# A four-layer graph-attention kernel: which products share a PSUM bank in layer 1, and in which round layer 2 takes a tile's last products

## The chip, the cores and the metric

The kernel runs on one core of a Trainium2 chip. The metric is the device time of one execution in microseconds (us); one measurement of this kernel is the median over several executions. The core has five engines with instruction streams of their own: TensorE (PE, with its weight loads shown apart as PEld), VectorE (DVE), ScalarE (ACT), GpSimd (POOL) and SyncE (SP). SP, ACT and POOL also issue DMA transfers. [...]

## The reference

Four graph layers act on `x` with 4096 nodes of 256 features. The adjacency matrix is sparse: each pair of nodes is joined with a chance of about 0.1% in either direction, made symmetric, with a loop at every node, so that a node has some nine neighbours. Each layer is residual and starts with a layer norm and a relu:

```python
h = jnp.maximum(_layernorm(x, axis=-1), 0.0)
x = x + layer(h, adj, ...)
```

- Layer 0: `h @ W.T` in 8 heads; a softmax over the neighbours of `leaky_relu(e_l[i] + e_r[j])` plus a bias from curvature features; the weighted sum of the neighbours' rows.
- Layer 1: one head. `e = a1·h[i] + a2·h[j]`, leaky relu, softmax over the neighbours, weighted sum of the neighbours' rows.
- Layer 2: as layer 1, but with two softmaxes, one over `e` and one over `-e`. Both weighted sums of the rows are concatenated, multiplied with `wtrans` (512x256) and passed through elu.
- Layer 3: four heads of 64 features. `h = x @ W + b`, the score of a pair is `leaky_relu(h[i]·h[j])`, absent edges score 1.0 and stay in the softmax; then relu.

## The kernel before, in words

**Tiles and lists.** The 4096 nodes are 32 tiles of 128 rows. A first stage turns the adjacency matrix into lists. For every tile there are nine chunks of 128 neighbour rows (`EC`), and one-hot matrices `st` that say which edge goes to which row of the tile. A layer keeps one row per node in a table in DRAM (`table0` to `table3`), which holds what the next layer needs of a node.

**Gathers.** The function `run` (L1698) works a layer through, tile by tile. For each tile POOL issues one indirect DMA for each chunk (`gather`, L914), which fetches 128 rows of the table into the buffer `g`. Six buffers exist (L827), so POOL runs up to six tiles ahead of the products that read them. The tile's own 128 rows come by an ordinary DMA from SP. The lists are sorted so that the first seven chunks touch the first 28 tiles' rows only (`NE` = 3584): these "early" gathers of the next layer can start when the rows of tiles 0 to 27 are in the table. The remaining chunks are "late" and need the whole table. In layers 1 and 3 the last chunk isn't gathered: TensorE expands it from rows kept in SBUF (`expanded`, L1682), with a one-hot matrix `to`, twelve matmuls and a copy by ACT into `g` (L1692). So POOL issues 9 gathers a tile in layers 0 and 2, and 8 in layers 1 and 3.

**Rounds.** `run` is given a list of steps, each with a lag. In round r, a step with lag k handles tile r - k; in a round the steps stand in the order of the list. TensorE executes in exactly this order. The instructions of the other engines are put in order by a scheduler, each engine's queue then being fixed in the program.

**Layer 1.** Its steps are: `loads` of tile r+3, which calls `go_to`; then gathers; `give2` of tile r-3; `weigh1` of r; `finish1` of r-2; `attend1` of r-1 (`summed`, L934 to L943, which frees the buffer `g`); `turn2` and `rows2` of r-2; `before1` of r+1; `expand1` of r+1. The small products are these. `go_to` (L1674) spreads a column of indices over 128 columns in PSUM, which DVE compares with row numbers (L1677) to give `to`. `give` (L908 in `to_edges`) sends a tile's own coefficients to its edges: nine matmuls of 3 columns, which DVE sums up (L1752). It is called for layer 1's coefficients (`before1`) and for layer 2's (`give2`). The PSUM tile "pm" of `ps_m` (one buffer) takes both `give`s; the tile "pe" of `ps_e` (one buffer) takes `go_to` and `expanded`. A PSUM tile is one bank, and a user waits for the last reader of the user before.

**Layer 2.** For a tile t, `weigh2` makes the two weight matrices (DVE L1872 and around), `attend2` multiplies them with `g` (28 matmuls a tile, L1894), `signed2` scales, `turn_signed` and `through_wt` multiply with `wtrans` (L1916, L1929), `finish2` gives the new `x` and its centred row `r`. Then come a tile's last products: `turn3` transposes `r` (L863) and ACT copies it to `hT` (L865); `rows3` multiplies `hT` with layer 3's weights (four matmuls, L872), DVE forms the row (L1957), and after every second tile ACT issues a store of two tiles' rows to `table3` (`store_two`, L774). `rows3` also splits the row in three bfloat16 parts, stores them in `own3`, and sums up squares on ACT (L1970). The order in a round is: `weigh2` of r, `signed2` of r-1, `finish2` of r-2, `attend2` of r, `turn3` of r-2, `turn_signed` of r-1, `rows3` of r-2, `before2` of r+1, `through_wt` of r-1.

**Layer 3.** POOL's queue first holds 42 early gathers (seven for each of the first six tiles), then late ones. The first of all waits for the store of tiles 26 and 27 to `table3`. `weigh3` needs all chunks of its tile (L2025, L2031, L2052, L2064), and `attend3` (again `summed`, L934 to L943) frees the buffer for the seventh tile's gathers.

Of the kernel before, what the change touches and what calls it, by code (L numbers as in the profile page):

```python
# [20 lines left out]
P = 128  # L21
# [675 lines left out]
EC = 9  # L697
# [16 lines left out]
def gnn_lists(  # L714
# [29 lines left out]
    NT = N // P  # L744
# [77 lines left out]
    own = [const.tile([P, NT, 3], F32, name=f"own{i}") for i in (1, 2)]  # L822
# [32 lines left out]
    def bank(pool, name, dtype=F32):  # L855
        t = pool.tile([P, 512], F32, name=name)
        return t if dtype == F32 else t.bitcast(dtype)
# [18 lines left out]
    def upper(a):  # L876

        n = len(a.shape)
        two = a.bitcast(BF16)
        if n == 2:  # L880
            return two.rearrange("p (a two) -> p a two", two=2)[:, :, 1]
        return two.rearrange("p s (a two) -> p s a two", two=2)[:, :, :, 1]
# [22 lines left out]
    def to_edges(pe, st, parts):  # L905

        for c in range(EC):
            nc.tensor.matmul(  # L908
                pe[:, c, :], lhsT=st[:, c * P : (c + 1) * P], rhs=parts, start=True, stop=True
            )  # L910
# [43 lines left out]
    with tc.tile_pool(name="keep", bufs=1) as keep, tc.tile_pool(  # L954
# [97 lines left out]
        at = keep.tile([P, NT], F32, name="at")  # L1052
# [573 lines left out]
    with tc.tile_pool(name="work", bufs=2) as work, tc.tile_pool(name="kept", bufs=1) as kept, tc.tile_pool(  # L1626
# [10 lines left out]
        def s_chunks(st):  # L1637

            pt = ps_s.tile([P, EC + 7, P], BF16, name="s_ps")[:, :EC, :]
            for c in range(EC):  # L1640
                nc.tensor.transpose(pt[:, c, :], st[:, c * P : (c + 1) * P], ident_b)  # L1641
            return pt
# [6 lines left out]
        def weights():  # L1649
            return work.tile([P, 2 * (HC + 2) * P], F32, name="sw")  # L1650
# [6 lines left out]
        def in_parts(parts, row, rest):  # L1657
            nc.scalar.copy(parts[0], row)
            nc.vector.tensor_sub(rest, row, parts[0])
            nc.scalar.copy(parts[1], rest)  # L1660
            nc.vector.tensor_sub(parts[2], rest, parts[1])

        def keep_late(rows, width):

            for b in range(0, LB, 2):
                n = min(LB, b + 2) - b
                row = rows[b // 2 - (LB + 1) // 2][:, 2 - n :, :]
                rest = work.tile([P, 2, ROW1], F32, name="rest", bufs=1)[:, :n, :width]
                in_parts([late_rows[:, b : b + n, i, :width] for i in range(3)], row, rest)

        def go_to(t, to):

            pm = bank(ps_e, "pe")[:, :P]
            nc.tensor.matmul(  # L1674
                pm, lhsT=col_late[:, t : t + 1].to_broadcast([P, P]), rhs=ident, start=True, stop=True
            )
            nc.vector.tensor_tensor(  # L1677
                to.rearrange("p (b e) -> p b e", b=LB), pm[:, None, :].to_broadcast([P, LB, P]),
                late_no[:, :, None].to_broadcast([P, LB, P]), op=OP.is_equal,
            )  # L1680

        def expanded(t, of, width, pool, name):  # L1682

            to = of.pop("to")
            ps = bank(pool, name)[:, :width]
            for b in range(LB):
                for i in range(3):
                    nc.tensor.matmul(  # L1688
                        ps, lhsT=to[:, b * P : (b + 1) * P], rhs=late_rows[:, b, i, :width],
                        start=(b == 0 and i == 0), stop=(b == LB - 1 and i == 2),  # L1690
                    )
            nc.scalar.copy(of["g"][:, LATE, :width], ps)  # L1692

        def store_x(dst, t, of):
            if t % XT == XT - 1:
                store(rows_of_x(dst, t + 1 - XT), of.pop("all_x"))
# [48 lines left out]

        a2_of = kept.tile([P, NT, EC + 1], F32, name="a2_of")

        def give(a, st, own_t):

            pe = bank(ps_m, "pm")[:, : EC * 3]  # L1750
            to_edges(pe.rearrange("p (c s) -> p c s", c=EC), st, upper(own_t))
            nc.vector.tensor_reduce(a[:, :EC], pe.rearrange("p (c s) -> p c s", c=EC), AX.X, OP.add)  # L1752
            nc.scalar.copy(a[:, SELF:], own_t[:, 0:1])

        def scores(g, a):
            s = work.tile([P, EC + 1], F32, name="s")
            with ExitStack() as queue:
                for step in behind.values():
                    queue.enter_context(tc.issue_after(step.ins))
                nc.vector.tensor_add(s, g[:, :, C + 1], a)  # L1760
            nc.vector.scalar_tensor_tensor(s, s, 0.2, s, op0=OP.mult, op1=OP.max)
            return s

        with tc.tile_pool(name="l1_o", bufs=2, space=PSUM) as ps_o, tc.tile_pool(
            name="l1_t", bufs=2, space=PSUM
        ) as ps_t, tc.tile_pool(name="l1_e", bufs=1, space=PSUM) as ps_e:
            for b in range(LB):
                nc.vector.tensor_scalar(
                    late_no[:, b : b + 1], number, float(NE + b * P), None, op0=OP.add
                )  # L1770
            nc.vector.tensor_copy(col_late, nbr[:, :, LATE])
            keep_late([rows12[t // 2 % len(rows12)] for t in range(0, NT, 2)], ROW1)

            def expand1(t, of):
                expanded(t, of, ROW1, ps_e, "pe")

            def before1(t, of):
                a = of["a"] = work.tile([P, EC + 1], F32, name="a")
                give(a, of["st"], own[0][:, t, :])
                of["s"] = s_chunks(of["st"])  # L1780

            def give2(t, of):
                give(a2_of[:, t, :], of.pop("st"), own[1][:, t, :])

            def weigh1(t, of):
                s = scores(of["g"], of.pop("a"))
                w = work.tile([P, EC + 1], F32, name="w")
                nc.scalar.activation(w, s, AF.Exp)
                sw = of["sw"] = weights()[:, : (EC + 1) * P].rearrange("p (c r) -> p c r", r=P)
                nc.vector.tensor_mul(  # L1790
                    sw[:, :EC, :], of.pop("s"), w[:, :EC, None].to_broadcast([P, EC, P])
                )
                nc.vector.tensor_scalar(
                    sw[:, SELF, :], ident, w[:, SELF:], loop[:, t : t + 1], op0=OP.mult, op1=OP.mult
                )

            def attend1(t, of):
                sw, g = of.pop("sw"), of.pop("g")
                o = of["o"] = bank(ps_o, "o")[:, : C + 1]
                summed(o, sw, g, C + 1, [(sw[:, SELF, :], g[:, SELF, : C + 1])])  # L1800

            def finish1(t, of):
                o, x = of.pop("o"), of.pop("x")
                nc.vector.reciprocal(inv[1][:, t, :], o[:, :1])
                nc.vector.scalar_tensor_tensor(
                    x, o[:, 1:], inv[1][:, t, :], x, op0=OP.mult, op1=OP.add
                )
                nc.vector.tensor_add(x, x, bias1)
                of["r"], of["rstd"] = normed(work, x)
                store_x(xs[1], t, of)  # L1810

            def turn2(t, of):
                of["hT"] = transposed(work, ps_t, of["r"])

            def rows2(t, of):
                rstd = of.pop("rstd")
                row = rows12[t // 2 % len(rows12)][:, t % 2, :]
                nc.scalar.activation(row[:, 1 : C + 1], of.pop("r"), AF.Copy, scale=rstd)
                pp = times(ps_t, of.pop("hT"), wcat2, 2)
                nc.vector.tensor_scalar(row[:, C + 1 :], pp[:, :1], rstd, None, op0=OP.mult)  # L1820
                nc.vector.tensor_scalar(own[1][:, t, 0:1], pp[:, 1:], rstd, None, op0=OP.mult)
                if t % 2:
                    store_two(table2, t, rows12[t // 2 % len(rows12)])
                split_own(own[1], t, 1)

            run(
                table1, ROW1, xs[0],
                [
                    (3, give2), (0, weigh1), (2, finish1), (1, attend1), (2, turn2), (-1, before1),
                    (2, rows2), (-1, expand1),  # L1830
                ],
                first=True, expand=True,
            )
# [15 lines left out]
        with tc.tile_pool(name="l2_o", bufs=1, space=PSUM) as ps_o, tc.tile_pool(  # L1849
# [93 lines left out]

            rows3_of = []

            def turn3(t, of):
                of["hT"] = transposed(work, ps_t, of.pop("r"))

            def rows3(t, of):
# [19 lines left out]
                for k in range(K3):  # L1969
# [4 lines left out]
            run(  # L1974
                table2, ROW1, xs[1],
                [
                    (0, weigh2), (1, signed2), (2, finish2), (0, attend2), (2, turn3), (1, turn_signed),
                    (2, rows3), (-1, before2), (1, through_wt),
                ],
            )  # L1980

# [213 lines left out]
```

## Time and profile before

| what | us |
|---|---|
| median of 14 runs | 1616.87 (1610.12 to 1620.17) |
| the profiled execution's own time | 1618.42 |
| its span | 1616.7 |
| first gather of layer 1, 2, 3 | 524.2, 853.33, 1217.54 |
| last gather of layer 2 | 1215.68 |
| last gather of layer 3 | 1554.89 |

The profile is of one execution, and all its times count from the start of the span; 1.7 us of the execution's time lie around it. An engine's group of instructions is given by line, operation, and tiles, with busy time and the idle time before it. "issue" as the cause of an idle time means that the engine waited for nothing that the profile shows. For an indirect DMA, POOL's bar is the time to issue it; the data land later. The mean clock granted to TensorE was 0.876 of full speed.

### The profile page before, as it was taken

The page shows a single profiled execution, that of the slowest core. Times are in us where ns is not written, and L with a number is a line of the kernel's source. Part 1 is how long each engine was busy: PE and PEld are TensorE (multiplying, and loading weights), DVE is VectorE, ACT ScalarE, POOL GpSimd, SP SyncE. Part 2 cuts the span into 40 slices and gives each one's busy share as a digit, 9 for nine tenths or more (in the row PEclk, how much of TensorE's full clock was granted, in tenths as well). Part 3 has the DMA queues.
Part 4 walks back from the last instruction along what each step waited for, and adds up shares of the span by engine and source line. Part 5 has one row for each costly group of instructions (what it writes and reads, how often), then busy time and mean ns, then how long its engine had stood idle before and what let it go on. Part 6 is the DMA issues. An engine that isn't in the chain of part 4 may idle for free.

```text
span 1616.7 us, 28902 instructions
## 1 busy us (share of the span) xinstructions
PE 1271.9 (79%) x9569; PEld 929.5 (57%) x9584; DVE 1091.1 (67%) x2979; ACT 763.5 (47%) x2246; POOL 1057.0 (65%) x1145
## 2 busy tenths in 40 slices
PE   4674788877888649988874499999997588888885
PEld 3342455545556337665553488888886355555553
DVE  5666778788877547765643266777665477888885
ACT  4565667776454334433321044444444344554543
POOL 2027766765666767777777777777777577777730
PEclk9975877787789769989796799999998699999998
DMA  8879888998556747877676467677767456666620
GB/s 267 293 246 321 286 287 288 324 306 255 131 150 170 221 138 226 242 204 198 205 228 183 127 195 206 194 210 213 207 207 214 147 175 196 195 205 198 212 78 16
DMA packets 167342, 338.02 MB, mean 209 GB/s; under 512 B 31761, under 2 KB 103697, under 8 KB 167185
## 3 DMA queue, kind: packets, MB, share of 16 engines
q0 software_dynamic: 52224, 145.30, 33.9%
q1 hardware_dynamic: 67714, 134.54, 24.8%
q10 hardware_dynamic: 47246, 56.27, 10.0%
q8 instruction: 77, 1.26, 0.3%
q14 instruction: 81, 0.66, 0.1%
HBM read 282.22 MB, written 53.77 MB: 208 GB/s over the span
## 4 chain that ended last, share of the span: by engine, by line
PE 31%; DMA 6%; POOL 6%; issue 5%; DVE 5%; ACT 2%; DVEq 0%; ACTq 0%; POOLq 0%; SPq 0%
PE o L1894 11%; DMA g<-table,nbr 6%; POOL g L914 6%; PE o L934 4%; PE pv L2025 3%; PE pt L1929 3%; PE o L939 3%; DVE v L2031 2%; PE pt L872 2%; PE o L943 1%; PE s_ps L1641 1%; PE pt L1916 1%; ACT y L2081 1%; PE pe L1688 0%; PE pt L863 0%
## 5 line engine op out<-in xcount | busy, mean ns | idle before, releaser
L914 POOL DMA_INDIRECT g<-table,nbr x1088 | 1042.4, 958 | 406.3 <-issue 308.9
L1894 PE MATMUL o<-g,sw 128*128 128x257 f32 x896 | 201.4, 382 | 36.6 <-DVE sw L1872 35.4
L1894 PEld LDWEIGHTS o<-g,sw 128*128 128x128 f32 x896 | 170.6, 191 | 62.0 <-DVE sw L1872 35.7
L2025 PE MATMUL pv<-parts,st 64*128 64x256 bf16 (+1 forms) x864 | 93.9, 288 | 67.4 <-DVE v L2031 65.4
L1192 ACT ACTIVATE mask<-adj,minus_half 128x1024 bf16<-128x1024 int32 x112 | 125.1, 1142 | 14.7 <-DMA adj<-in_adj_l 5.1
L2025 PEld LDWEIGHTS <-st 64*128 64x128 bf16 (+1 forms) x864 | 57.3, 99 | 101.0 <-issue 93.8
L2081 ACT ACTIVATE y<-o,inv 128x64 f32<-128x64 f32 x128 | 36.0, 312 | 164.1 <-DVE inv L2077 164.1
L872 PE MATMUL pt<-wcat,hT 128*128 128x272 f32 (+2 forms) x384 | 95.0, 365 | 13.8 <-ACT hT L865 11.8
L2031 DVE TENSOR_TENSOR v<-pv,g 128x512 f32<-128x512 f32 (+1 forms) x160 | 93.2, 630 | 17.9 <-DMA g<-table,nbr 12.3
L939 PE MATMUL o<-g,sw 128*64 128x257 f32 (+1 forms) x768 | 102.0, 402 | 0.0
L865 ACT COPY hT<-pt 128x256 f32<-128x256 f32 x128 | 46.9, 367 | 112.8 <-PE pt L863 109.4
L896 ACT ACTIVATE off<-place,minus 128x1152 bf16<-128x1152 f16 x64 | 80.0, 1251 | 37.5 <-DVE st L897 36.9
L1641 PE MATMUL s_ps<-ident_b,st 128*128 128x128 bf16 x864 | 66.7, 225 | 36.2 <-DVE sw L1790 36.2
L863 PE MATMUL pt<-ident,r 128*128 128x128 f32 x256 | 56.1, 305 | 46.1 <-DVE r L843 15.0
L1531 DVE TENSOR_TENSOR g<-g,pb 128x2560 f32<-128x2560 f32 x32 | 90.0, 2813 | 3.4 <-ACT pb L1528 3.3
L2064 DVE TENSOR_TENSOR g<-g,pm 128x2048 f32<-128x2048 f32 x32 | 73.2, 2288 | 25.8 <-ACT pm L2057 25.7
L934 PE MATMUL o<-g,sw 128*128 128x257 f32 (+1 forms) x320 | 89.6, 414 | 0.0
L1688 PEld LDWEIGHTS <-st 128*128 128x128 bf16 x768 | 80.3, 109 | 15.3 <-issue 1.6
L1641 PEld LDWEIGHTS <-st 128*128 128x128 bf16 x864 | 56.7, 100 | 46.3 <-DVE sw L1790 24.0
L2052 DVE TENSOR_REDUCE s<-v 128x36 f32<-128x2304 f32 x32 | 81.7, 2553 | 1.1
L872 PEld LDWEIGHTS pt<-wcat,hT 128*128 128x128 f32 x384 | 65.0, 204 | 28.9 <-ACT hT L865 16.3
L1499 ACT CAST s_f<-pt 128x1024 f32<-128x1024 bf16 x64 | 37.8, 642 | 92.8 <-PE o L943 92.4
(363 smaller groups left out, 2716.5 us busy)
## 6 DMA issues: line engine op xcount, KB each, us to landing
adj<-in_adj_l SPq DMA_DIRECT2D x128, 512.0 KB
g<-table,nbr POOLq DMA_INDIRECT x1088
rows_of<-st ACTq DMA_DIRECT2D x16, 832.0 KB
st<-rows_of SPq DMA_DIRECT2D x16, 832.0 KB
x<-x SPq DMA_DIRECT2D x24, 512.0 KB
st<-rows_of SPq DMA_DIRECT2D x16, 576.0 KB
table<-row ACTq DMA_DIRECT2D x32, 258.0 KB
g<-table SPq DMA_DIRECT2D x64, 129.0 KB
```

The costliest lines, as they stand in the source:

```text
L872: nc.tensor.matmul(pp, lhsT=hT[:, k, :], rhs=w[:, k, :], start=(k == 0), stop=(k == KC - 1))
L914: nc.gpsimd.indirect_dma_start(out=g[:, c, :width], out_offset=None, in_=table[: NE if c < EARLY else N, :], in_offset=bass.IndirectOffset ...
L934: nc.tensor.matmul(o, lhsT=a, rhs=b, start=(i == 0), stop=False)
L939: nc.tensor.matmul(o[rows], lhsT=s[:, c + h * HC, rows], rhs=g[:, c + h * HC, :width], start=False, stop=False,)
L1192: nc.scalar.activation(m, a, AF.Sign, bias=minus_half, scale=1.0)
L1531: nc.vector.tensor_mul(gh, gh, w[:, :, :, None].to_broadcast([P, K, H0, D0]))
L1641: nc.tensor.transpose(pt[:, c, :], st[:, c * P : (c + 1) * P], ident_b)
L1688: nc.tensor.matmul(ps, lhsT=to[:, b * P : (b + 1) * P], rhs=late_rows[:, b, i, :width], start=(b == 0 and i == 0), stop=(b == LB - 1 and i ...
L1894: nc.tensor.matmul(o, lhsT=sw[:, h, i].rearrange("p s r -> p (s r)"), rhs=g[:, c, : C + 1], start=(i == 0), stop=(i == HC + 1),)
L2025: nc.tensor.matmul(to, lhsT=st[r, c * P : (c + 1) * P], rhs=parts[r, i, :], start=(i == 0), stop=(i == 2),)
L2031: nc.vector.tensor_mul(v[:, chunks, :], pv, g[:, chunks, :C])
L2052: nc.vector.tensor_reduce(s[:, :EC, :], heads(v, K3), AX.X, OP.add)
```

## The change

There are two edits, independent of each other.

In layer 1, one PSUM tile "pm" is taken in each round, by `go_to`, and all three small products of the round write to places of their own in it: `go_to` columns 0 to 127, `before1`'s `give` 27 columns from 128 on, `give2`'s the 27 after those. "pe" is left to `expanded` alone. A round with no `go_to` goes on using the last tile.

In layer 2, `turn3` and `rows3` get a lag of 3 in place of 2 for tiles 0 to 29, and keep 2 for the last two tiles; and `turn3` moves ahead of `attend2` in the round.

```diff
+        round_ = []
+
         def go_to(t, to):
-            pm = bank(ps_e, "pe")[:, :P]
+            round_[:] = [bank(ps_m, "pm")]
+            pm = round_[0][:, :P]
             nc.tensor.matmul(
                 pm, lhsT=col_late[:, t : t + 1].to_broadcast([P, P]), rhs=ident, start=True, stop=True
             )
...
-        def give(a, st, own_t):
-            pe = bank(ps_m, "pm")[:, : EC * 3]
+        def give(a, st, own_t, at):
+            pe = round_[0][:, at : at + EC * 3]
             to_edges(pe.rearrange("p (c s) -> p c s", c=EC), st, upper(own_t))
...
             def before1(t, of):
                 a = of["a"] = work.tile([P, EC + 1], F32, name="a")
-                give(a, of["st"], own[0][:, t, :])
+                give(a, of["st"], own[0][:, t, :], P)
...
             def give2(t, of):
-                give(a2_of[:, t, :], of.pop("st"), own[1][:, t, :])
+                give(a2_of[:, t, :], of.pop("st"), own[1][:, t, :], P + EC * 3)
...
+            def turn_lag(t):
+                return 3 if t < NT - 2 else 2
...
                 [
-                    (0, weigh2), (1, signed2), (2, finish2), (0, attend2), (2, turn3), (1, turn_signed),
-                    (2, rows3), (-1, before2), (1, through_wt),
+                    (0, weigh2), (1, signed2), (2, finish2), (turn_lag, turn3), (0, attend2),
+                    (1, turn_signed), (turn_lag, rows3), (-1, before2), (1, through_wt),
                 ],
```

## The prediction

> **What bounds the kernel now.** I read the page's busy shares and costliest groups first, then POOL's timeline at the borders of the layers, busy times by window, and last the chain of waits. Part 1 and part 5 of the page:
>
> ```profile
> PE 1271.9 (79%) x9569; PEld 929.5 (57%) x9584; DVE 1091.1 (67%) x2979; ACT 763.5 (47%) x2246; POOL 1057.0 (65%) x1145
> ...
> L914 POOL DMA_INDIRECT g<-table,nbr x1088 | 1042.4, 958 | 406.3 <-issue 308.9
> ```
>
> PE looks like the bound, but 1042.4 + 308.9 of "issue" make 1351 us in which POOL does nothing but issue gathers: 0.95 + 0.30 = 1.25 each. POOL's timeline (start, duration, operation, idle time before it):
>
> ```profile
> 583.40 0.99 POOL L914 DMA_INDIRECT g<-table,nbr  x1 [0.30 <-issue]
> 591.32 0.94 POOL L914 DMA_INDIRECT g<-table,nbr  x1 [6.92 <-PE pm L908]
> ...
> 1215.68 0.95 POOL L914 DMA_INDIRECT g<-table,nbr  x1 [0.30 <-issue]
> 1217.54 0.94 POOL L914 DMA_INDIRECT g<-table,nbr  x1 [0.91 <-DVE r L843]
> ...
> 1277.22 0.95 POOL L914 DMA_INDIRECT g<-table,nbr  x1 [0.30 <-issue]
> 1288.56 0.94 POOL L914 DMA_INDIRECT g<-table,nbr  x1 [10.39 <-PE o L943]
> ```
>
> POOL stops once in layer 1, 6.67 over its turn of 1.25, for the seventh tile's buffer. From 591.32 to 1277.22 it stops only once more, for 0.61 at 1217.54. It alone paces layers 1 and 2: 8 gathers a tile are 10.02 us, 9 are 11.27. Windows in mid-layer 1 and 2 (length; PE, PEld, DVE, ACT, POOL; clock, DMA share, GB/s):
>
> ```profile
> 600.00:640.00 40.00, 37.18 (x353) 28.04 (x354) 29.42 (x96) 16.26 (x48) 30.34 (x32) 0.96 0.72 211
> 940.00:980.00 40.00, 39.90 (x219) 34.13 (x218) 27.62 (x80) 19.56 (x80) 30.25 (x33) 1.00 0.70 201
> ```
>
> At 600 PE catches up at 7.37 us a round (`go_to`'s product at 604.17 and 611.54), then waits for data. In layer 2 it is full from 907.8 on, at 10.05 a round, still below POOL's 11.27; it catches up by 1190 and waits for gathers again. In layer 3, PE, DVE and POOL take turns in rounds of 10.05 to 10.3 that begin with tile 0. How they begin, from the chain of waits (start, duration, what ran):
>
> ```profile
> 1270.98 2.72 DMA g<-table,nbr
> ...
> 1274.84 2.56 DVE s L2052
> ...
> 1281.99 3.46 PE o L934 x8
> ...
> 1288.56 2.53 DMA g<-table,nbr
> ```
>
> The gather issued at 1270.98 is tile 0's late one, the 43rd in POOL's queue. Everything in layer 3 follows it, so layer 3 starts when POOL's first gather of `table3` does.
>
> **What sets that first gather.** It waits for the `table3` store of tiles 26 and 27. The timelines of PE, DVE and ACT there:
>
> ```profile
> 1209.40 1.13 PE L872 MATMUL pt<-w_s,hT 128*128 128x256 f32 x4 [0.51 <-ACT hT L865]
> ...
> 1213.25 6.23 PE L1894 MATMUL o<-g,sw 128*128 128x257 f32 x28
> ```
> ```profile
> 1210.57 0.48 DVE L1957 SCALAR_TENSOR_TENSOR row<-pt,rstd,b_s 128x256 f32<-128x256 f32 x1 [0.24 <-PE pt L872]
> ...
> 1219.64 0.17 DVE L1760 TENSOR_TENSOR s<-g,a_of 128x10 f32<-128x10 f32 x1 [2.52 <-DMA g<-table,nbr]
> ...
> 1221.84 0.48 DVE L1957 SCALAR_TENSOR_TENSOR row<-pt,rstd,b_s 128x256 f32<-128x256 f32 x1 [0.35 <-PE pt L872]
> ```
> ```profile
> 1211.08 0.37 ACTq L774 DMA_DIRECT2D table<-row  x1
> ```
>
> Tile 27's product is at 1209.40, its row at 1210.57, the store at 1211.08, its last landing at 1216.9 and the gather at 1217.54: 6.46 after the store's issue, 0.61 after POOL's own turn. The store has no spare time at all.
>
> **What the Trainium skill says.** "PSUM — Partial Sum Buffer", section "PSUM bank collisions raise a hardware error", tells to guard PSUM by bank, not by address: products in different columns of "pm" still wait for one another's readers. No run here shows a collision; in the changed program's order these waits stand. Section "Engine vs sequencer instructions" has DVE, ACT and POOL as strict FIFOs and matmuls in program order; the trace agrees (DVE stood 12.26 us at L2031 for the late gather). "DMA: Bandwidth & Descriptors", section "Anatomy of one DMA — SWDGE (gpsimd) path", says a DMA's semaphore comes only after its last byte is confirmed, slowest to HBM, and fits 2.0 us + bytes/436e3. For 258 KB that is 2.6, an estimate; four `table3` stores landed here in 3.4, 5.1, 5.5 and 5.8, so the trace is used.
>
> **Layer 2's edit, step by step.** No instruction is added. Per tile two transposes (L863), the copy to `hT`, four matmuls (L872), the row, three parts, sums and, every second tile, two stores come one round later. What it removes is PE's wait for ACT's copy, from the view of waits (sum, count, largest), 900 to 1220:
>
> ```profile
> PEld pt L872 <- ACT hT L865: 7.8, 28, 0.8
> ```
>
> PE's own share of it is 0.5, and POOL paces the layer: worth 0. What it costs: tile 27 has lag 3, so its `rows3` falls in round 30, behind `attend2(30)` on PE (1213.25 to 1219.48) and, on DVE, behind `weigh2(31)`, which waits for the last gather (1219.64). It takes the place where now tile 28's row is, at 1221.84. As `hT` is long there, the idle 0.35 before that row goes: 1221.49, against 1210.57. The store moves +10.9. Behind it on ACT nothing of note waits; on POOL all of layer 3's gathers do. `own3`'s store moves too, and with it the fetch of layer 3's first parts (1231.1, used from 1257: hidden, 15 to spare). The last rows of layer 2 end near 1256 as before and are needed at 1271 or later. POOL's queue keeps its order; SP's loads of `x` and `st` move by places that nothing waits for.
>
> Store to gather took 6.46. With that again, the first gather is 10.9 later. But by then the layer's last gathers have landed and the queues are emptier: with the fastest landing seen, 3.4 for 5.8, it is 2.4 less. I take the middle, 9.7; ends 10.9 and 8.5 (7.7 with the 2.6).
>
> **Layer 1's edit.** It removes `go_to`'s wait for `expanded`'s copy by ACT; 600 to 840:
>
> ```profile
> PEld pe L1674 <- ACT g L1692: 23.5, 26, 1.6
> PE pe L1674 <- ACT g L1692: 14.9, 26, 1.3
> ```
>
> That is 14.9 / 32 = 0.47 a round on PE. It adds, per round, a wait of `give2`'s first product for DVE's comparison (L1677, 0.69 once begun), of `before1`'s `give` for `give2`'s sum (L1752, 0.18), and of the next `go_to` for `before1`'s sum. Queued behind these on PE is the rest of the round, `attend1` included. These cost between nothing (done before PE comes) and 1.4 (all of 0.69 + 0.18 + 0.18, and 0.35 of hand-over); I take 0.9, as `give2` follows `go_to` closely. Less the 0.47 that is +0.4: a round of 7.8, ends 6.9 and 8.3. Cover: POOL's 10.02; all of it is hidden. In the changed order L1677 also stands ahead of the round's gather wait on DVE (L1760), so it doesn't inherit that wait. If the cover were gone, POOL would stop once PE is more than four tiles behind.
>
> Not hidden is the layer's start, where POOL waits 6.67 for `attend1(0)`. There the comparison (0.60) moves ahead of DVE's gather wait, and `go_to(4)` no longer waits 0.46 plus some of the copy: about 1.2 earlier, between 0 and 1.8. From 591.32 on POOL has no slack up to layer 2's last gather, so it reaches 1215.68, and DVE's 1219.64 with it.
>
> **Sum.** +9.7 - 1.2 = +8.5 on the profiled 1618.42 is 1626.9. That execution is 1.55 above the median of 14, so I forecast 1616.87 + 8.5 = 1625.4. Ends: +7.7 - 1.8 = +5.9 (1622.8) and +10.9 - 0 (1627.8); with the executions' own scatter, 1621.5 to 1629.5.
>
> **Rivals.**
>
> *The late start is swallowed.* POOL stands 10.1 us before its gather at 1288.56. If `attend3(0)`, which frees that buffer, hung on something other than POOL's 43rd gather, a later start would only fill this gap, up to 10.1, and only layer 1's 1.2 would be left, if that carries: 1615.7, not slower. It decides on what DVE waited for at 1273.78; the trace names the gather, with 12.26 us of idle DVE before it and 0.08 after its landing. Chance 0.10.
>
> *The shared bank paces layer 1.* If DVE's queue puts the comparison behind a gather wait after all, each round holds a gather's landing in PE's order. At 10.5 a round instead of 10.02, tile 31 comes 15 later; the store of tile 27 (issued 839.59, landed 843.6, needed 853.33) has 9.7 spare, so 5 more: 1630 and up. Against it stand 2.2 us of slack per round. Chance 0.07.
>
> *Part of the delay is lost elsewhere*, such as a shorter stop at 1288.56 or earlier rows of tile 27: 1618 to 1621.5, chance 0.05. That the layer-2 edit fails to remove PE's wait changes nothing, as the wait is hidden.
>
> **How the numbers follow.** The main case has 0.78. The range 1621 to 1630 leaves out the first rival and most of the second. About 0.2%, 3.2 us, is what a measurement can tell. The first rival gives 0.08 same and 0.02 faster, the third 0.02 same, the rest is slower.
>
> **What would show it.** Right: PE's L872 for tile 27 after `attend2(30)`, near 1219 to 1220; its row after the last gather's L1760; the store near 1221; the first gather of layer 3 near 1226 with POOL idle some 10 before it; POOL's stop before the seventh tile still about 10; POOL's first stop in layer 1 near 5.5; L1674 without a wait for ACT. Wrong: a first gather still near 1217, a stop before tile 6 of layer 3 that shrinks by the delay, or POOL gaps between 600 and 840.

## The result and the profile after

The changed kernel takes 1629.12 us (median of 10 runs, 1623.87 to 1632.68) against 1615.01 us for the kernel before (47 runs, 1610.12 to 1620.17): a ratio of 1.0084, 95% interval 1.0071 to 1.0096. By that ratio it is 13.6 us slower (11.5 to 15.5); the medians alone differ by 14.1. The forecast was 1625.4 in a range of 1621 to 1630, with a loss of 8.5. The sign, the place and the path of the delay were right. The loss was not: it lies above 10.9, the upper end of the forecast's own sum. That the time is inside the range is in part luck, since the kernel before has 1615.01 here, where the forecast started from 1616.87; from there the same loss would have given 1630.4.

The profiled execution took 1628.24 us with a span of 1626.5. Part 1 and the costliest group of its page:

```profile
PE 1253.6 (77%) x9569; PEld 925.9 (57%) x9584; DVE 1088.7 (67%) x2979; ACT 764.6 (47%) x2246; POOL 1059.9 (65%) x1145
...
L914 POOL DMA_INDIRECT g<-table,nbr x1088 | 1044.5, 960 | 415.6 <-issue 309.2
```

No engine's busy time grew by more than 0.3%. What grew is POOL's idle time, and POOL's timeline has it in one place:

```profile
579.23 0.95 POOL L914 DMA_INDIRECT g<-table,nbr  x1 [0.30 <-issue]
586.49 0.94 POOL L914 DMA_INDIRECT g<-table,nbr  x1 [6.31 <-PE pm L908]
...
1212.99 0.95 POOL L914 DMA_INDIRECT g<-table,nbr  x1 [0.30 <-issue]
1228.12 0.94 POOL L914 DMA_INDIRECT g<-table,nbr  x1 [14.18 <-DMA g<-table]
...
1287.54 0.95 POOL L914 DMA_INDIRECT g<-table,nbr  x1 [0.30 <-issue]
1298.56 0.94 POOL L914 DMA_INDIRECT g<-table,nbr  x1 [10.08 <-PE o L943]
```

Over its turn of 1.25, POOL stands 6.0 in layer 1 (6.7 before), 13.9 ahead of layer 3's first gather (0.6 before), and still 9.8 ahead of the seventh tile's gathers (10.1 before). The late start was not swallowed by that last stop. (At 1228.12 the column names a load that landed at the same time; by the program the gather waits for the store of tiles 26 and 27.) The timelines of the other engines at the border, PE and DVE first, then the queues of ACT and SP:

```profile
1212.84 6.23 PE L1897 MATMUL o<-g,sw 128*128 128x257 f32 x28
...
1219.34 1.03 PE L872 MATMUL pt<-w_s,hT 128*128 128x256 f32 x4
```
```profile
1207.67 0.17 DVE L1763 TENSOR_TENSOR s<-g,a_of 128x10 f32<-128x10 f32 x1 [3.08 <-DMA g<-table,nbr]
...
1216.76 0.17 DVE L1763 TENSOR_TENSOR s<-g,a_of 128x10 f32<-128x10 f32 x1
...
1220.41 0.48 DVE L1964 SCALAR_TENSOR_TENSOR row<-pt,rstd,b_s 128x256 f32<-128x256 f32 x1 [0.87 <-PE pt L872]
```
```profile
1220.93 0.41 ACTq L774 DMA_DIRECT2D table<-row  x1
```
```profile
1220.90 0.32 SPq L1712 DMA_DIRECT2D st<-rows_of  x1
1221.83 7.50 SPq L927 DMA_DIRECT2D g<-table  x5
```

Tile 27's product stands behind `attend2(30)`, as forecast, and its row goes to the table at 1220.93. In the same instant SP starts an 832 KB load of one-hot matrices for layer 3 and then, ahead of the first gather, four of 128 KB (the fifth of that line is issued at 1229.01). From the store's issue to the first gather it is 7.2 us. In the kernel before, that big load is issued at about the same time, but the store and the first gather lie ahead of it:

```profile
1222.34 0.32 SPq L1709 DMA_DIRECT2D st<-rows_of  x1
```

So it is the store that moved next to the load. What follows that gather has the length it had: to the end it is 399.2 us before and 398.4 after.

The waits that the two edits set out to remove are gone. PE's matmuls and weight loads no longer wait for `hT` in layer 2 or for ACT's copy into `g` in layer 1. In layer 1 the shared bank has waits of its own (600 to 840; sum, count, largest):

```profile
PE pm L908 <- DVE st L1680: 19.5, 25, 0.8
PE pm L908 <- DVE a_of L1755: 14.7, 4, 5.3
```

The second kind stood in the kernel before too, and shorter:

```profile
PE pm L908 <- DVE a_of L1752: 3.9, 4, 1.8
```

POOL does not stop between 600 and 840 in either kernel, so these waits are hidden.

### The profile page after: what moved, and what is told of

Same layout as the page of the kernel before. It is cut to its first block, busy times and chain, and to the rows that moved or that the text cites. A ratio compares the mean times of both kernels' runs of the same rounds, so it can differ in the third digit from the quotient of the medians.

```text
span 1626.5 us, 28940 instructions
## 1 busy us (share of the span) xinstructions
PE 1253.6 (77%) x9569; PEld 925.9 (57%) x9584; DVE 1088.7 (67%) x2979; ACT 764.6 (47%) x2246; POOL 1059.9 (65%) x1145
## 3 DMA queue, kind: packets, MB, share of 16 engines
q8 instruction: 77, 1.26, 0.3%
## 4 chain that ended last, share of the span: by engine, by line
PE 45%; DVE 14%; DMA 11%; POOL 10%; issue 8%; ACT 6%; DVEq 0%; ACTq 0%; POOLq 0%
PE o L1897 11%; POOL g L914 10%; DMA g<-table,nbr 10%; PE o L934 8%; PE o L939 6%; PE pt L1932 4%; PE pv L2032 3%; PE o L943 2%; DVE v L2038 2%; PE pt L872 2%; PE s_ps L1641 2%; PE pe L1691 1%; PE pt L863 1%; DVE g L1531 1%; ACT s_f L1499 1%
## 5 line engine op out<-in xcount | busy, mean ns | idle before, releaser
L1897 PE MATMUL o<-g,sw 128*128 128x257 f32 x896 | 201.0, 381 | 35.1 <-DVE sw L1875 33.9
L1897 PEld LDWEIGHTS o<-g,sw 128*128 128x128 f32 x896 | 168.0, 190 | 58.9 <-DVE sw L1875 34.2
L1192 ACT ACTIVATE mask<-adj,minus_half 128x1024 bf16<-128x1024 int32 x112 | 125.1, 1142 | 15.7 <-DMA adj<-in_adj_l 7.0
L934 PE MATMUL o<-g,sw 128*128 128x257 f32 (+1 forms) x320 | 85.8, 400 | 0.0
```

What stands on the lines that cost most here:

```text
L934: nc.tensor.matmul(o, lhsT=a, rhs=b, start=(i == 0), stop=False)
L1192: nc.scalar.activation(m, a, AF.Sign, bias=minus_half, scale=1.0)
L1897: nc.tensor.matmul(o, lhsT=sw[:, h, i].rearrange("p s r -> p (s r)"), rhs=g[:, c, : C + 1], start=(i == 0), stop=(i == HC + 1),)
```

## The experiments

Where an experiment has layer 2's edit alone, the loss to compare with is that of the second run. Each ratio is to the kernel before on the same chip, and a loss or gain in us that is given with it is worked out from the ratio. The diffs are cut to their core; those of `turn_lag` are taken against layer 2's edit.

**Each edit alone.** The first run has layer 1's edit without layer 2's, the second the reverse.

> Layer 1's edit alone, layer 2 as before. Theory (tile 27's store is the whole cost): no loss, between -1.2 and +1 us against before (1614 to 1616 on a before of 1615.0), layer 3's first gather again some 6.5 us after a store that lies ahead of layer 2's last gather, PE's round at the start of layer 1 at 7.4 to 7.9 us. Rival (the shared bank costs what the forecast missed): +3 to +5 us, with more POOL gaps between 590 and 840 us than before.

> Layer 2's edit alone, layer 1 as before. Theory: the whole loss, +11 to +14 us, with POOL standing about 13 us before layer 3's first gather and again about 10 us before the seventh tile's. Rival (the shared bank has a part of it): +8 to +10 us.

Layer 1's edit alone: 1614.14 against 1615.86, ratio 1.000 (0.9986 to 1.0013). Layer 2's alone: 1629.33, ratio 1.0086 (1.0068 to 1.0104), the same as both together. The whole loss is layer 2's. In the profile of the first run PE's round at the start of layer 1 is 7.59 us (`go_to`'s product at 606.48 and 614.07), against 7.37; POOL's stop there is 5.9 over its turn, against 6.7. So the new waits cost 0.2 a round more than the removed one, hidden as forecast, and the earlier start is worth 0.8, less than a timing can show.

**The last rows left where they were.** Two runs try to keep the edit for most tiles and the store of tiles 26 and 27 in its old round. The first only ends the longer lag at tile 25:

```diff
-                return 3 if t < NT - 2 else 2
+                return 3 if t < NT - 6 else 2
```

> Layer 2's edit alone with the lag of 3 for tiles 0 to 25 only, so that tiles 26 and 27 are stored in the round they were stored in before; layer 1 as before. Theory: the loss is gone, within 1.5 us of before, POOL's stop before layer 3's first gather under 2 us. Rival (the later products cost something in layer 2 itself): most of the loss stays, +5 us or more.

1623.33 us, ratio 1.0056 (1.0036 to 1.0077): 9.1 us more than before. That is the rival's number, but not for the rival's reason, as one more run shows, with the transposes moved ahead and lag 2 for every tile:

> Only the transposes moved ahead of the weighted sums in layer 2's round, lag 2 for all tiles; layer 1 as before. Theory: within 1 us of before, since PE's wait for the copy was hidden behind POOL's gathers. Rival (the removed wait is worth something): -1 to -4 us.

1779.39 us, ratio 1.1021 (1.0998 to 1.1045), far outside both. PE's timeline in layer 2 and its waits from 950 to 1320 in that run:

```profile
1010.38 0.41 PE L863 MATMUL pt<-ident,r 128*128 128x128 f32 x2 [4.10 <-DVE r L843]
```
```profile
PE pt L863 <- DVE r L843: 85.9, 22, 4.1
```

With lag 2, a tile's transposes stand right behind the products from which DVE makes `r`; before, `attend2`'s 6.2 us lay between and covered DVE's work. Moved ahead, they make PE stand 4.1 us in nearly every round, with `attend2` queued behind. So the move is only free with the longer lag. The other half, the longer lag with the transposes left behind the weighted sums, was not run. In the run before it, tiles 26 to 31 have exactly this fault (PE waits 3.7 and 4.4 for `r` at 1193.08 and 1210.00), so their products come late although their lag is the old one: the store of tiles 26 and 27 is issued 8.6 us behind layer 2's last gather (4.6 ahead of it before), and POOL stands 10.4 over its turn. A late store cost time there too, but the run did not put it back. The next run leaves the last tiles in their old order too:

```diff
-                    (0, weigh2), (1, signed2), (2, finish2), (0, attend2), (2, turn3), (1, turn_signed),
-                    (2, rows3), (-1, before2), (1, through_wt),
+                    (0, weigh2), (1, signed2), (2, finish2), (turn_lag, turn3_early), (0, attend2),
+                    (turn_lag, turn3_late), (1, turn_signed), (turn_lag, rows3), (-1, before2),
+                    (1, through_wt),
```

Here `turn3_early` does tiles 0 to 25, `turn3_late` the others, and the lag is 3 for tiles 0 to 25.

> Layer 2's edit alone for tiles 0 to 25 (lag 3, transposes ahead of the weighted sums); tiles 26 to 31 exactly as before (lag 2, transposes behind the weighted sums). Layer 1 as before. Theory (the loss is the late store of tiles 26 and 27, and nothing in the rounds before it): within 2 us of before, POOL's stop ahead of layer 3's first gather at 0.6 to 2 us. Rival (the later products of all the other tiles cost something): +4 us or more.

1616.51 us against 1614.38, ratio 1.0008 (0.9994 to 1.0021): the loss is gone, to within 3 us. POOL's stop ahead of layer 3's first gather is 2.5 over its turn, a little more than expected:

```profile
1217.96 0.95 POOL L914 DMA_INDIRECT g<-table,nbr  x1 [2.81 <-DMA g<-table]
```

The later products of the other 26 tiles cost nothing and bring nothing that can be measured. The cost lies in the last six tiles; that among these it is the store of tiles 26 and 27 is read from the profiles.

**One round later still.**

```diff
-                return 3 if t < NT - 2 else 2
+                return 4 if t < NT - 4 else 3 if t < NT - 2 else 2
```

> Layer 2's edit alone with a lag of 4 for tiles 0 to 27, 3 for 28 and 29, 2 for the last two: tile 27's row comes one more round later. Theory (layer 3 starts with that store, one for one): about 10 us on top of layer 2's edit, 22 to 26 us above before, layer 3's first gather near 1238 to 1242. Rival (a start that is late by more is swallowed by POOL's later stop of 10 us): +13 to +17 us.

1632.39 us, ratio 1.0099 (1.0079 to 1.0119): 16.0 us more than before (12.8 to 19.2). That is short of the theory's 22 and inside the rival's 13 to 17, but the rival's reason does not hold: POOL's stop ahead of the seventh tile is 8.9 over its turn, against 9.2 in layer 2's edit alone, so it swallowed nothing that can be seen. In the profile the store lies 10.2 us later after layer 1's start than with lag 3 (713.1 against 703.0), as expected, but the gather follows after 3.2 us in place of 6.6, so layer 3's first gather is only 6.7 later. Neither expectation had that. At the store's time no other load starts:

```profile
1227.29 0.32 SPq L1709 DMA_DIRECT2D st<-rows_of  x1
1227.92 1.54 SPq L927 DMA_DIRECT2D g<-table  x3
```
```profile
1237.44 0.37 ACTq L774 DMA_DIRECT2D table<-row  x1
```
```profile
1240.60 0.95 POOL L914 DMA_INDIRECT g<-table,nbr  x1 [20.61 <-DVE low L1937]
```

The end in this profile is 7.4 us later after layer 1's start than with lag 3, but the profiled execution was the slowest of its five, and the times put it 2 us above lag 3, with an interval of some 4 to either side. So this run doesn't settle by its times whether a later start is paid one for one; the last run below does better.

**What the store waits for.** The 3.2 us point to the loads that start beside the store. Two runs above say the same. In the one with lag 3 to tile 25, only one load of 128 KB is issued near the store, 1.8 us ahead of it, and the gather follows after 3.0:

```profile
1219.96 0.37 ACTq L774 DMA_DIRECT2D table<-row  x1
```
```profile
1223.00 1.01 POOL L914 DMA_INDIRECT g<-table,nbr  x1 [10.67 <-DVE low L1937]
```

In the one with the order alone it is 3.1. The traces' records of DMA packets show where the rest of the time goes. In the four profiles with 3.0 to 3.2 us, the store's 256 packets of 1 KB run from 0.9 to 1.8 us after its issue. In the ten others the first of them starts after 2.3 to 3.3 and the last ends after 4.3 to 5.7. In all of them the gather follows 1.3 to 1.8 us behind the last packet. So the store's packets themselves come late where other transfers run.

Two runs move loads. The first missed the one beside the store:

```diff
+                    if expand and not first and t == 4:
+                        with tc.issue_after(store_of["27"].ins):
+                            nc.scalar.dma_start(
+                                of[t]["sts"][:, :, :whole], rows_of[t // 2][:, :, :whole]
+                            )
```

> Layer 2's edit alone, and the 832 KB load of one-hot matrices that starts in the same instant as the store of tiles 26 and 27 is put behind that store on the same queue. Theory (the two share the DMA engines, and so the store takes 6.6 us to the gather where the forecast had 5.3): 4 to 4.8 us from the store's issue to the first gather, 1.5 to 2.5 us less than layer 2's edit alone. Rival (the store's own completion takes that long): 6 us or more, no gain.

1625.52 us, ratio 1.0061 (1.0041 to 1.0081), and 6.7 us from the store to the gather. The load beside the store is that of tiles 6 and 7; this edit took that of tiles 4 and 5, which used to start 22 to 24 us earlier, and so put a second one beside it. Its time lies 4 us below layer 2's edit alone, with an interval of some 4 to either side; even if that is a gain, it isn't the expected one. Nothing follows from it on the store's time, other than that a second load queued behind the store made it no slower. Its first gather was earlier for another reason: the store was issued 6.0 us after layer 2's last gather, not 9.3, since tile 30's gather landed sooner. The moved load no longer ran beside that gather (more on this below).

The right load, held back:

```diff
+                        if expand and not first and t == 6:
+                            queue.enter_context(tc.issue_after(behind_sp["parts3"].ins))
```

> Layer 2's edit alone, with SyncE's 832 KB load of one-hot matrices for layer 3's tiles 6 and 7, which starts in the same instant as the store of tiles 26 and 27, held back on SyncE's queue behind a later load. Theory (store and load share the DMA engines): 3 to 4.5 us from the store's issue to layer 3's first gather, in place of 6.6 to 7.2, and 2 to 3.5 us less than layer 2's edit alone (some 1625.5 to 1627 on a before of 1615). Rival (the store takes that long by itself behind layer 2): 6 us or more, no gain.

This run and two more, marked below, come from a chip on which the kernel before takes 2281.27 us; their times are compared only with that. The ratio is 0.9989 (0.9967 to 1.0011). The time from store to gather is what was asked. With the load held, from the queue of ACT and the timeline of POOL:

```profile
1753.07 0.37 ACTq L774 DMA_DIRECT2D table<-row  x1
```
```profile
1756.11 1.17 POOL L915 DMA_INDIRECT g<-table,nbr  x1 [46.43 <-DVE low L1943]
```

That is 3.0 us. The next run below, on the same chip and with the load where it was, has:

```profile
1755.44 0.32 SPq L1709 DMA_DIRECT2D st<-rows_of  x1
```
```profile
1755.46 0.41 ACTq L774 DMA_DIRECT2D table<-row  x1
```
```profile
1761.96 0.94 POOL L914 DMA_INDIRECT g<-table,nbr  x1 [54.13 <-DMA g<-table]
```

That is 6.5 us, and the third run on that chip has 6.8. So the loads double the store's time. Holding the first one also let four of the five small ones behind it go ahead of the store, and the fifth went after it, so their shares aren't told apart. What that brings on the other chips was not measured: on this one the two kernels with layer 2's edit (this and the next) are not measurably slower than the kernel before.

**Why the row itself came later than forecast.** The edit moves the store of the split rows of tiles 24 and 25 next to the store of `x`. This run puts it behind the stores of tiles 26 and 27:

> Layer 2's edit alone, with the store of the split rows of tiles 24 and 25, which the edit moves next to the store of x and the last gathers of tile 30, put behind the stores of tiles 26 and 27. Theory (that store slows tile 30's last gather, so that the whole of round 30 and with it tile 27's row come later than the forecast had them): tile 30's weights begin 7 us or more ahead of layer 2's last gather instead of 5.3, the store of tiles 26 and 27 is issued 6 to 7.5 us after that gather instead of 7.9 to 9.3, and 1 to 3 us less than layer 2's edit alone. Rival (the landing of that gather differs by itself between executions): no change of the median.

The ratio is 0.998 (0.9955 to 1.0006). On that chip the store of tiles 26 and 27 comes 44 to 49 us after layer 2's last gather was issued, and tile 30's gather has long landed, so the run says nothing on the question. What the other profiles say on it stands with the sum below.

**Layer 3's first late gather earlier.** In the kernel before, tile 0's late gather is 43rd in POOL's queue. Here tile 4's early gathers stand behind it:

```diff
+                with ExitStack() as queue:
+                    if expand and not first and t == 4:
+                        queue.enter_context(tc.issue_after(behind_pool["late"].ins))
+                    of[t]["g"] = gather_early(t, table, width, g_pool)
```

> Before, with one change in POOL's queue at the start of layer 3: the early gathers of tile 4 come behind tile 0's late gather, which moves from the 43rd place to the 29th. Theory (layer 3 starts with that gather): it is issued at about 1256, as soon as the table is complete, VectorE's wait of 12.3 us before its first product with it goes, and the end comes 8 to 12 us earlier. Rival (layer 3's start hangs on something else, such as the last rows of layer 2): no gain, within 2 us.

1599.41 us, ratio 0.9903 (0.9883 to 0.9924): 15.7 us less than the kernel before (12.4 to 18.9), more than expected, and faster than both kernels. POOL's timeline there:

```profile
1248.58 0.95 POOL L916 DMA_INDIRECT g<-table,nbr  x1 [0.30 <-issue]
1251.68 0.95 POOL L916 DMA_INDIRECT g<-table,nbr  x1 [2.15 <-DMA g<-table]
```

The late gather goes at 1251.68, earlier than the 1256 expected, after 1.85 us of waiting for the table. DVE no longer waits for it. POOL has no other stop over 0.3 us up to the last gather: the 10 us ahead of the seventh tile and the smaller stops behind it are gone, and POOL alone paces layer 3 (321.3 us from the first gather to the last, 255 steps of 1.26).

The changed kernel with the same change ran on two chips, first on the slow one:

> The changed kernel (both edits) with tile 0's late gather ahead of tile 4's early ones at the start of layer 3, as in the run of the kernel before with that one change. Theory (POOL's gathers then pace all of layer 3 from its first one, so that a late start is paid one for one): 12 to 14 us over that run, about 1612, with no stop of POOL before the seventh tile. Rival (with the slack found there the late store no longer matters): within 3 us of it, about 1600.

The ratio there is 0.9941 (0.9917 to 0.9965), which cannot be set beside 1612. And then:

> The changed kernel with tile 0's late gather ahead of tile 4's early ones at the start of layer 3, once more, since the first run of it fell on a chip on which every kernel takes 1.4 times as long. Theory (POOL's gathers then pace layer 3 from its first one, and a late start is paid one for one): 12 to 14 us over the kernel before with that same change (1599.4), so about 1612, no stop of POOL before the seventh tile. Rival (the late store no longer matters): about 1600.

1611.31 us against 1615.64, ratio 0.9974 (0.9962 to 0.9986). The two edits thus cost 0.0071 or 11.5 us on top of the late gather's move, with about 4 to either side, as expected. POOL stops 13.7 us over its turn ahead of layer 3's first gather and no more ahead of the seventh tile:

```profile
1232.28 0.94 POOL L916 DMA_INDIRECT g<-table,nbr  x1 [13.99 <-DMA g<-table]
```

Within that interval the late store is paid in full also where POOL has no later stop.

## Why the prediction was right, and where its sum was off

**Which layer, which wait.** Right. POOL's gathers pace layers 1 and 2; both removed waits were hidden; layer 3 starts with the store of tiles 26 and 27; the delay goes through to the end. The profiles bear out "one for one" to within 4 us: from layer 3's first gather to the end it is 395.5 to 399.2 us in the nine profiles of chips other than the slow one that keep POOL's queue, while that gather lies between 1215.5 and 1240.6 in eight of them and at 1381.6 in the run with the order alone.

**The rivals.** The swallowed start fell: the stop of 10.1 us is 9.8 with the late store, and in the nine profiles it lies between 7.6 and 10.1 without following the start. What released DVE decided it, as the prediction said; DVE's wait for tile 0's late gather grew from 12.26 to 23.39. Moving that gather is what removed the stop. The shared bank as a pace fell with the first run. The third rival, a part of the delay lost elsewhere, fell with the measured time, which is later and not earlier than the main case.

**The sum.** Its terms, taken in the profiles from layer 1's first gather on, since what lies before differs by up to 6 us between executions and neither edit reaches it:

| term | predicted | after | layer 2's edit alone |
|---|---|---|---|
| layer 1's first gather to layer 2's last | -1.2 | +1.5 | +2.1 |
| layer 2's last gather to the store | +10.9 | +12.5 | +13.9 |
| store to layer 3's first gather | -1.2 | +0.7 | +0.1 |
| layer 3 from there to the end | 0 | -0.8 | -3.4 |
| sum | +8.5 | +14.0 | +12.8 |

Three terms were mis-sized, and all on the same side. (The -3.4 in the fourth row is no effect of the edit: layer 1's edit alone has -3.5 there.) For the second of them, this is `weigh2(30)` in the kernel before; its line after stands above, at 1207.67:

```profile
1208.28 0.17 DVE L1760 TENSOR_TENSOR s<-g,a_of 128x10 f32<-128x10 f32 x1 [2.26 <-DMA g<-table,nbr]
```

- "But by then the layer's last gathers have landed and the queues are emptier": this step failed. The gathers were gone, but the wait that had held SP's load (PE's last transposes of `st`, at 1220.21) ends beside the store's own. The prediction looked at what would be finished and not at what would be released. Alone the store needs 3.0 to 3.2 to the gather. The 3.4 to the landing that the prediction named would be 4.1 to the gather; its 2.6 was an estimate from a fit for transfers of POOL, and this store is ACT's. With the loads it needed 6.6 to 7.2. Price: 1.3 to 1.9 us.
- "It takes the place where now tile 28's row is, at 1221.84": its place is right, but the wait named was not. DVE's `weigh2(31)` found its gather landed (no idle time at 1216.76). The row waited for PE, whose `attend2(30)` began 0.15 us before POOL's last gather, not 2.43 as before, because tile 30's gather had landed 5.3 us ahead of it, not 7.4. Price: 1.6 to 3.0 us. That landing goes with the transfers beside it. It is 5.2 to 5.5 us ahead of POOL's last gather in four profiles (the changed kernel, the same with the late gather moved, layer 2's edit alone, the last rows as before). In these, tiles 24 and 25 have lag 3, and their stores of 256 and 384 KB are issued 10 to 15 us ahead of that last gather, as is an 832 KB load. It is 6.7 to 7.4 ahead in four others (the kernel before, the same with the late gather moved, layer 1's edit alone, lag 4). There the load is issued some 1 to 2 us earlier, and the two stores some 11 us earlier or, with lag 4, later. In the run that put a second load beside the store, just that 832 KB load had been taken away from here: the gather had landed 8.1 ahead, and the store came 10.6 later than before, about the forecast 10.9. So the transfers that the edit moves next to tile 30's gather are the likely cause. This is not shown: the run made for it fell on the slow chip, and it moved only one of the two stores.
- Layer 1's start: the stop is 5.9 to 6.0 over its turn in the three profiles with layer 1's edit and 6.4 to 6.7 in the eight without it, on chips other than the slow one: some 0.6 less, not 1.2. The gain is lost in the scatter of the stretch from layer 1's first gather to layer 2's last, which is 2.9 and 3.2 us longer than before in two runs without that edit. That scatter lies in the gathers themselves: POOL's busy time for the 544 of them is 520.4 us before and up to 523.5 in the other runs without stops in layer 2.

**The round of layer 1.** Forecast 7.8, measured 7.59; the wait for the comparison is 0.78 in 25 rounds (19.5 / 25), where all added waits were taken at 0.9, and what it replaces was 0.57 in 26 (14.9 / 26). The next most likely added wait, for DVE's sums, shows in four rounds only.

**What the prediction passed over.** It counted of the transposes' move ahead of `attend2` only the hidden wait that it removes, and never said that the move is free because of the longer lag; nor did the expectation for the order alone, which missed 10%.

## What to carry to other kernels

Where one queue paces two layers in a row, the instruction that lets it into the second layer has no slack, however much slack its engine has in the middle of the first: a lag that is free for 26 tiles cost 13.6 us in the last few, by the profiles for the one pair on which the next layer waits. When a transfer moves, list what else is released at its new time, not only what will be done by then; and when an order and a lag are changed together, ask what each would cost without the other. The place of a single gather in a queue (43rd or 29th) was worth 15.7 us, about as much as the change under study.

## What the runs showed of the hardware

A store of 256 KB took 3.0 to 3.2 us from its issue to the first gather waiting for it when no load of one-hot matrices and no gather ran beside it (four profiles), and 6.1 to 7.2 us in the ten others, before and after among them. The difference is in its packets: they ran from 0.9 to 1.8 us after the issue in the four, and ended after 4.3 to 5.7 us in the ten.

And one chip differed from the others by more than any change here: on it, the kernel before took 2281 us against 1615. The three profiles of that chip show POOL's gather at 0.95 us as elsewhere, and PE's matmuls in L1897's place at 389 to 390 ns against 381 to 382 before and after. The mean granted clock is 0.77 to 0.78 there, against 0.88, and POOL's idle time ahead of its gathers is 1045 to 1070 us, against 406 and 416. Why is open. There, two kernels with layer 2's edit and one more change each had 0.9989 and 0.998 of the time before.
